# A graph layer on one core: packed adjacency masks turned by VectorE in 32x32 blocks, with row groups in the quadrants

## The chip, the cores and the metric

The kernel runs on one core of one Trainium2 chip. The metric is device time in microseconds (us), from the first to the last thing the program does; the median of three runs before the change is 190.73 (190.70 to 190.74). A core has five engines that work at the same time, each through its own queue in order: PE (TensorE, matrix multiplication), DVE (VectorE), ACT (ScalarE), POOL (GpSimd) and SP (SyncE, which here only issues DMAs).

## The reference

Inputs are `x` (4096 x 64), an adjacency matrix `adj` (4096 x 4096, float32, zeros and ones), a weight (64 x 64) and a bias (64).

```python
h = jnp.maximum(_layernorm(x, axis=-1), 0.0)
support = h @ weight
mask = (adj != 0).astype(support.dtype)
rank = jnp.cumsum(mask, axis=1)
deg = rank[:, -1:]
k = jnp.minimum(deg, 100.0)
pos = rank - (deg - k)
w = mask * jnp.where(pos > 0, 0.5 ** (k - pos), 0.0)
out = x + (w @ support + bias)
```

Since `k - pos = deg - rank`, the weight of a neighbour is one half to the power of the number of neighbours to its right in the row, and zero from the hundredth on. So for each row the kernel counts ones from the right, makes a weight of each, and multiplies by `support`. `adj` is 67.1 MB and is read once.

## The kernel before

**Units.** The 4096 rows are 32 row tiles of 128 (a tile takes every sixteenth row of one half of the matrix, so that each partition's x rows are contiguous). Four row tiles make a row group `g` of W = 512 rows, and each group is done in two column halves of 2048 columns, the right one first: 16 units, 64 loads of 1 MB (`load`, L115, a ring of NA = 8 buffers of 8 KB a partition).

**From mask to weights.** For each load, `convert` (L330) turns float32 into bytes 64 or 65 and puts four columns into one 32-bit word: DVE does 61 of 64, ACT three. `transpose` (L344) turns the words, 128 x 128 at a time, on PE into PSUM, four per load; `settle` (L354) copies them back to SBUF on DVE. Columns are now on the partitions, rows on the free axis, 512 rows side by side. For each unit, `totals` (L365, eight matmuls into 32-row strips) counts the ones of blocks of columns; the count comes as two bytes, which `split` (ACT, L378) and `divide` (DVE, L381) take out; for a left half, `carry` (POOL, L387) adds what the right half found; `suffix` (L390, two matmuls) sums over the blocks to the right; `clamp` (DVE, L398) limits the sum. `place` (L402) makes, for four PSUM banks at a time, the exponents of all columns: four matmuls of 32 rows with `where`, then sixteen of 32 x 32 with the triangle `tri`. `weigh` (ACT, L415) takes an exponential of two bytes of each word: 128 x 1024 weights from one bank. `aggregate` (L445) multiplies them into a 128 x 512 accumulator, two matmuls of 512 columns per weigh, with `support` split into a high and a low part (`hr`) as the stationary side.

**Ends.** `drain`, `turn_back` and `finish` (L462 to L486) add the bias, turn a row group back, add x in SBUF. In the last unit three weighs are done by DVE instead (`encode`, `take`, with `lower` on POOL and `gather` on PE) and three are cut into halves of 256 rows. Two large stores wait for all loads to be issued; the last two go out from ACT's and SP's queues.

**Set-up.** x is turned (`turn`, `turned`), normalised (`center`, `square`, `relu`, `spread`, `root`, `power` on POOL), multiplied by the weight (`support`), scaled (`scale`), split (`first`, `second`). `warm` gives PE matmuls without use, where a planned gap is long.

**Order.** A planner at the end of the function (L524 to L657) holds for each step its engine, a rank (with hand-set shifts), an assumed hold and lag, what it needs and which pool it takes a buffer from; it places the steps one by one, and each engine's queue is written in that order. The order is fixed when the program is built; at run time each instruction waits for its own semaphores. PSUM has two banks for counts and turns (NB), five for `place` (NV) and one for the accumulator.

Of the kernel before, what the change touches and what calls it, by code (L numbers as in the profile page):

```python
# [29 lines left out]

@with_exitstack
def kernel(
# [14 lines left out]

# [7 lines left out]
    CB = HB // E  # L74
# [4 lines left out]
    G = RT // TG  # L79

    UNITS = [(g, c * P * E, n) for g in range(G) for c, n in ((4, 4), (0, 4))]
    U = len(UNITS)
    UT = [(u, tt) for u in range(U) for tt in range(TG)]
    NT = len(UT)
    POS = [sum(UNITS[v][2] for v, _ in UT[:n]) // 2 for n in range(NT + 1)]
    NP = 2 * CB
    QUICK = (U - 2, 4), (U - 1, 0), (U - 1, 4)
    PARTED = 5, 6, 7
    NA = 8
    NV = 5  # L90
    NB = 2
# [4 lines left out]
    bpool = ctx.enter_context(tc.tile_pool(name="bpool", bufs=6))  # L96
    mpool = ctx.enter_context(tc.tile_pool(name="mpool", bufs=3))
    wpool = ctx.enter_context(tc.tile_pool(name="wpool", bufs=NP + 4))
    dpool = ctx.enter_context(tc.tile_pool(name="dpool", bufs=2))
    bhpool = ctx.enter_context(tc.tile_pool(name="bhpool", bufs=3))  # L100
# [7 lines left out]


    tiles = {}  # L110
    xt = mpool.tile([P, CB, W, 2], F16, name="mt").rearrange("p c i e -> p (c i e)").bitcast(F32)
    xr = const.tile([P, H, HT, D], F32, name="xr")
    xr_v = x.rearrange("(r p t) d -> p r t d", r=H, t=HT)

    def load(n):  # L115
        u, tt = UT[n]
        g, c0, cb = UNITS[u]
        t = g * TG + tt
        tiles[n] = apool.tile([P, N // H], F32, tag="a_sb", name="a_sb")
        nc.sync.dma_start(tiles[n][:, :cb * E * P], adj_v[:, t // HT, t % HT, c0:c0 + cb * E * P])  # L120
# [9 lines left out]

# [13 lines left out]

    thr, later, excess = {}, {}, {}
    for cb in sorted({cb for g, c0, cb in UNITS}):
        thr[cb] = setup.tile([P, 4, SUB], F32, name=f"thr{cb}")
        later[cb] = const.tile([P, 2, P], F16, name=f"later{cb}")
        excess[cb] = const.tile([P, 1], F32, name=f"excess{cb}")
        nc.gpsimd.memset(thr[cb], 4096.0)  # L150
        nc.gpsimd.iota(thr[cb][:, :, 4:4 + 4 * cb].rearrange("p j (a f c) -> p j a f c", f=2, c=4),
                       pattern=[[1, 4]] + [[32, 2]] * (cb == CB) + [[16, 2], [4, 4]], base=0, channel_multiplier=0,
                       allow_small_or_imprecise_dtypes=True)
        nc.gpsimd.memset(thr[cb][:, :, 0:1], -1.0)
# [21 lines left out]

# [11 lines left out]
    for q in range(4):  # L188
        nc.gpsimd.memset(band[q * SUB:(q + 1) * SUB, SUB - 4 + q:SUB - 3 + q], 1.0)
    over = setup.tile([P, 1], F16, name="over")  # L190
    nc.gpsimd.memset(over, 136.0)
    floor = const.tile([P, 1], F32, name="floor")
    nc.gpsimd.memset(floor, -38.0 * LN2)
# [4 lines left out]
    used = setup.tile([P, 2], F32, name="used")  # L198

    def order_of(cb):  # L200


        sub = setup.tile([P, 2], F32, name=f"sub{cb}")
        nc.vector.scalar_tensor_tensor(sub[:, 0:1], pf[:, 1:2], 8.0 if cb == CB else 2.0, pf[:, 3:4], op0=ALU.mult, op1=ALU.add)
        nc.vector.scalar_tensor_tensor(sub[:, 0:1], pf[:, 2:3], 0.125, sub[:, 0:1], op0=ALU.mult, op1=ALU.add)
        nc.vector.tensor_scalar(sub[:, 1:2], sub[:, 0:1], 16.0, None, op0=ALU.add)
        nc.vector.memset(sub[:1, 0:1], 4000.0)
        for f in range(2):
            nc.vector.tensor_scalar(later[cb][:, f, :], thr[cb].rearrange("p j r -> p (j r)"), sub[:, f:f + 1], used[:, f:f + 1],
                                    op0=ALU.is_lt, op1=ALU.mult)  # L210

    def constants(n):
        if n == 0:
            nc.vector.tensor_tensor(pi[:, 1:], pi[:, 0:1].to_broadcast([P, 5]), bits, op=ALU.bitwise_and)
            nc.vector.tensor_copy(pf, pi)
            nc.vector.tensor_scalar(used, pf[:, 5:6].to_broadcast([P, 2]), 8.0, None, op0=ALU.is_equal)
            nc.vector.memset(used[:1, 0:1], 1.0)

            nc.vector.tensor_scalar(one, row, 20.0, -1.0, op0=ALU.is_ge, op1=ALU.mult)
        elif n == 1:  # L220

# [15 lines left out]

    hr = const.tile([P, B, 2, D], F32R, name="hr")
    xs = setup.tile([P, B, D], F32, name="xs")
    sq = xs.rearrange("p (b s) d -> p b (s d)", s=2)  # L240
    rx = setup.tile([P, HB, P], F32, name="rx")
# [3 lines left out]
    def warm(n):  # L245

        for i in range(n):
            nc.tensor.matmul(none[:, :2 * P], junk[:, :P], junk, start=True, stop=True)  # L248

    pxs, sqs, ns = {}, {}, {}  # L250

    def turn(h, t0):

        pv = pxs[h, t0] = ps_v.tile([P, P, 4], F32, tag="v", name="px")
        for t in range(4):
            nc.tensor.transpose(pv[:D, :, t], xr[:, h, t0 + t, :], ident)  # L256
# [5 lines left out]
    def center(n):  # L262

        pxs[n] = ps_v.tile([P, W], F32, tag="v", name="pc")
        nc.tensor.matmul(pxs[n], less.rearrange("p h d -> p (h d)"), xt[:, n * W:(n + 1) * W], start=True, stop=True)  # L265


    def groups(of, n):
        return of[:, 4 * n:4 * n + 4, :].rearrange("p j (c l) -> p c j l", l=SUB)

    def square(n):
        nc.scalar.activation(groups(sq, n), pxs[n].rearrange("p (c j l) -> p c j l", c=4, j=4), AF.Square, scale=D ** -0.5)  # L272

    def relu(n):
        nc.scalar.activation(groups(rx, n), pxs.pop(n).rearrange("p (c j l) -> p c j l", c=4, j=4), AF.Relu)
# [8 lines left out]

# [7 lines left out]

# [17 lines left out]
    def piece(h, i):  # L310
        return slice(h * HB + i * HB // 2, h * HB + (i + 1) * HB // 2)

    def first(h, i):
        nc.scalar.activation(hr[:, piece(h, i), 0, :], xs[:, piece(h, i), :], AF.Copy)

    def second(h, i):
        nc.vector.tensor_sub(hr[:, piece(h, i), 1, :], xs[:, piece(h, i), :], hr[:, piece(h, i), 0, :].bitcast(F32))

    def count(cb):
        r = SUB * cb  # L320
        px = pxs["count", cb] = ps_v.tile([P, W], F32, tag="v", name="pn")
        nc.tensor.matmul(px[:, :1], later[cb][:r, 1, :], over[:r], start=True, stop=True)

    def counted(cb):
        nc.vector.tensor_scalar(excess[cb], pxs.pop(("count", cb))[:, :1], one, None, op0=ALU.add)


    low, codes, masks, words, wts, accs, tots, pts, sums8, behind, vs, signed = {}, {}, {}, {}, {}, {}, {}, {}, {}, {}, {}, (1, 7, 15)

    def convert(n):  # L330
        cb = UNITS[UT[n][0]][2]
        m8 = bpool.tile([P, CB * P, E], U8, name="m8")
        m_v, a_v = m8[:, :cb * P, :], tiles.pop(n)[:, :cb * P * E]
        if cb == CB:
            m_v, a_v = m_v.rearrange("p q e -> p e q"), a_v.rearrange("p (e q) -> p e q", e=E)
        else:
            m_v, a_v = m_v.rearrange("p q (a f) -> p a f q", f=2), a_v.rearrange("p (f a q) -> p a f q", f=2, a=2)
        if n in signed:
            nc.scalar.activation(m_v.bitcast(I8), a_v, AF.Sign)  # L339
        else:  # L340
            nc.vector.tensor_scalar(m_v, a_v, 0.0, 64.0, op0=ALU.not_equal, op1=ALU.add)  # L341
        words[n] = m8

    def transpose(n, c0, c1):  # L344
        u, tt = UT[n]
        if tt == 0 and c0 == 0:
            masks[u] = mpool.tile([P, CB, W, 2], F16, name="mt")
        if c0 == 0:
            pts[n] = ps_t.tile([P, CB, P], F32, tag="t", name="pt")
        m32 = words[n].rearrange("p q e -> p (q e)").bitcast(F32)  # L350
        for c in range(c0, c1):
            nc.tensor.transpose(pts[n][:, c, :], m32[:, c * P:(c + 1) * P], ident)  # L352

    def settle(n):  # L354
        u, tt = UT[n]
        cb = UNITS[u][2]
        mw = masks[u].rearrange("p c i e -> p c (i e)").bitcast(U32)[:, :cb, tt * P:(tt + 1) * P]
        pt = pts.pop(n).bitcast(U32)[:, :cb, :]
        words.pop(n)
        if n in signed:  # L360
            nc.vector.tensor_scalar(mw, pt, 0x01010101, 0x40404040, op0=ALU.bitwise_and, op1=ALU.bitwise_or)
        else:
            nc.vector.tensor_copy(mw, pt)  # L363

    def totals(u):  # L365
        tot = pts[u, "n"] = ps_t.tile([P, W], F32, tag="t", name="tot")
        for a in range(2):
            for c in range(UNITS[u][2]):
                nc.tensor.matmul(tot[SUB * c:SUB * (c + 1), :], band[:, SUB - 12 - 4 * a:2 * SUB - 12 - 4 * a],  # L369
                                 masks[u][:, c, :, a], start=(a == 0), stop=(a == 1), skip_group_check=True)  # L370

    def bytes_of(u, f):
        r = SUB * UNITS[u][2]
        if u not in sums8:
            sums8[u] = dpool.tile([P, 2, W], F16, name="sums8")
        return sums8[u][:r, f, :], pts[u, "n"][:r].bitcast(U8).rearrange("p (i f) -> p f i", f=4)[:, 1 + f, :]

    def split(u):  # L378
        nc.scalar.activation(*bytes_of(u, 0), AF.Copy)  # L379

    def divide(u):  # L381
# [313 lines left out]
```

## Time and profile before

| | |
|---|---|
| median of three runs | 190.73 us (190.70 to 190.74) |
| the profiled execution's own time | 190.5 us |
| its span, first to last instruction | 188.8 us |
| mean granted PE clock | 0.979 |
| busy PE / DVE / ACT / POOL | 171.8 / 161.7 / 149.5 / 20.4 us |
| read from memory / written | 68.19 MB / 1.05 MB |
| loads of adj | 64 of 1 MB, median 16.5 us from issue to landing |

Busy times are unions of instruction records; records of one engine overlap, since an instruction may begin before its predecessor has ended. The price of an instruction in a queue is therefore read from start to start of neighbours that waited for nothing. The 40 slices are 4.72 us each.

### The profile page before, as it was taken

How to read it: one execution, taken by the hardware profiler on the slowest of the kernel's cores; microseconds unless marked ns; L12 is line 12 of the kernel's file. 1: busy time of each engine (PE TensorE's matmuls, PEld its weight loads, DVE VectorE, ACT ScalarE, POOL GpSimd, SP SyncE). 2: the span in 40 equal slices, each digit the busy share in tenths (PEclk: the TensorE clock that was granted, in tenths of full speed). 3: DMA queues.
4: the chain of work that ended last, by engine and by line, in shares of the span. 5: the costliest groups of instructions: out<-in, count | busy, mean ns of one | idle time of the engine just before them, and what ended most of it. 6: DMA issues, size and time to landing. Idle time of an engine off the chain costs nothing.

```text
span 188.8 us, 3797 instructions
## 1 busy us (share of the span) xinstructions
PE 171.8 (91%) x1499; PEld 107.7 (57%) x1499; DVE 161.7 (86%) x221; ACT 149.5 (79%) x176; POOL 20.4 (11%) x60
## 2 busy tenths in 40 slices
PE   7879979898989999999979997999799999999980
PEld 5657746655555565466546554655366545554560
DVE  4834758899999999999999989998999899996743
ACT  2298055789899896999897889787978997899970
POOL 7000035020001000100020002000100029001000
PEclk9999687999999999999999999999999999999998
DMA  6999999999999999999999999999999999931000
GB/s 212 417 422 422 415 427 420 417 415 420 420 422 420 420 417 418 429 422 413 422 420 420 422 417 418 420 425 418 420 422 410 424 420 418 418 128 62 21 3 28
DMA packets 10338, 69.49 MB, mean 368 GB/s; under 512 B 1360, under 2 KB 1616, under 8 KB 2128
## 3 DMA queue, kind: packets, MB, share of 16 engines
q1 hardware_dynamic: 10016, 69.15, 88.6%
q8 instruction: 12, 0.20, 0.4%
q10 hardware_dynamic: 304, 0.10, 0.2%
q14 instruction: 6, 0.05, 0.1%
HBM read 68.19 MB, written 1.05 MB: 367 GB/s over the span
## 4 chain that ended last, share of the span: by engine, by line
PE 49%; DVE 29%; DMA 10%; ACT 5%; POOL 3%; issue 2%; POOLq 0%; ACTq 0%; DVEq 0%
PE acc L453 18%; DVE m L341 13%; DMA a_sb<-in_adj_dram 10%; PE pt L352 10%; DVE mt L363 6%; PE v L412 4%; PE v L407 4%; ACT wk L420 3%; PE pc L265 2%; PE tot L369 2%; PE pd L281 2%; PE ps L396 2%; DVE behind L400 2%; PE po L476 2%; ACT mt L260 1%
## 5 line engine op out<-in xcount | busy, mean ns | idle before, releaser
L420 ACT ACTIVATE wk<-v 128x1024 fp32r<-128x1024 uint8 (+1 forms) x128 | 120.0, 1015 | 15.3 <-PE v L412 14.9
L341 DVE TENSOR_SCALAR m<-a_sb 128x2048 uint8<-128x2048 f32 x61 | 84.9, 1394 | 4.2 <-DMA a_sb<-in_adj_dram 4.1
L453 PE MATMUL acc<-wk,hr 128*128 128x512 f32 (+1 forms) x256 | 77.7, 421 | 1.1 <-ACT acc_sb L469 0.6
L453 PEld LDWEIGHTS acc<-wk,hr 128*128 128x128 f32 x256 | 43.4, 189 | 18.6 <-issue 6.3
L352 PE MATMUL pt<-ident,m 128*128 128x128 f32 x256 | 41.2, 286 | 6.0 <-DVE m L341 5.4
L363 DVE COPY mt<-pt 128x512 uint32<-128x512 uint32 x61 | 41.7, 685 | 4.3 <-PE pt L352 4.3
L352 PEld LDWEIGHTS pt<-ident,m 128*128 128x128 f32 x256 | 29.7, 145 | 20.6 <-PE acc L453 4.8
L388 POOL COPY sums<-behind 1x512 f16<-1x512 f16 x8 | 6.8, 852 | 129.6 <-ACT sums L379 109.5
L407 PE MATMUL v<-behind,where 32*128 32x512 f16 x128 | 13.7, 383 | 1.5 <-DVE behind L400 1.1
L412 PE MATMUL v<-mt,tri 32*32 32x512 f16 x512 | 14.2, 394 | 0.0
L379 ACT ACTIVATE sums<-tot 128x512 f16<-128x512 uint8 x16 | 9.7, 608 | 3.5 <-PE tot L369 3.5
L400 DVE TENSOR_SCALAR behind<-ps,excess 128x512 f16<-128x512 f32 x16 | 11.9, 745 | 0.1
L382 DVE CAST sums<-tot 128x512 f16<-128x512 uint8 x16 | 10.9, 683 | 1.1 <-ACT sums L379 1.1
L369 PE MATMUL tot<-mt,band 128*32 128x512 f16 x128 | 10.2, 393 | 0.3 <-DVE mt L363 0.3
L396 PE MATMUL ps<-sums,later 128*128 128x512 f16 x32 | 10.0, 396 | 0.2 <-DVE sums L382 0.2
L407 PEld LDWEIGHTS <-where 32*128 32x128 f16 x128 | 3.7, 90 | 10.3 <-issue 9.8
L412 PEld LDWEIGHTS <-tri 32*32 32x32 f16 x512 | 4.4, 88 | 8.7 <-issue 8.7
L248 PE MATMUL none<-junk 128*128 128x256 bf16 x44 | 7.9, 362 | 1.1 <-DVE junk L133 1.1
L260 ACT ACTIVATE mt<-px 64x512 f32<-64x512 f32 x8 | 4.2, 585 | 4.9 <-PE px L256 4.8
L339 ACT ACTIVATE m<-a_sb 128x2048 int8<-128x2048 f32 x3 | 7.6, 2547 | 0.0
L248 PEld LDWEIGHTS <-junk 128*128 128x128 bf16 x44 | 5.6, 129 | 3.4 <-DVE junk L133 1.1
L272 ACT ACTIVATE xs<-pc 128x512 f32<-128x512 f32 x4 | 2.3, 610 | 6.0 <-PE pc L265 6.0
(87 smaller groups left out, 100.6 us busy)
## 6 DMA issues: line engine op xcount, KB each, us to landing
a_sb<-in_adj_dram SPq DMA_DIRECT2D x64, 1024.0 KB, 16.5
xr<-in_x_dram SPq DMA_DIRECT2D x2, 512.0 KB, 6.3
out_dram<-xr SPq DMA_DIRECT2D x1, 512.0 KB, 18.4
out_dram<-xr SPq DMA_DIRECT2D x1, 384.0 KB, 2.3
out_dram<-xr ACTq DMA_DIRECT2D x1, 64.0 KB, 1.6
out_dram<-xr SPq DMA_DIRECT2D x1, 64.0 KB, 1.7
w<-in_L_gnn_weight_dram ACTq DMA_DIRECT2D x2, 16.0 KB, 6.0
bias_sb<-in_L_gnn_bias_dram SPq DMA_DIRECT2D x1, 0.2 KB, 14.1
```

The lines of the kernel that those rows point to most:

```text
L248: nc.tensor.matmul(none[:, :2 * P], junk[:, :P], junk, start=True, stop=True)
L341: nc.vector.tensor_scalar(m_v, a_v, 0.0, 64.0, op0=ALU.not_equal, op1=ALU.add)
L352: nc.tensor.transpose(pts[n][:, c, :], m32[:, c * P:(c + 1) * P], ident)
L363: nc.vector.tensor_copy(mw, pt)
L369: nc.tensor.matmul(tot[SUB * c:SUB * (c + 1), :], band[:, SUB - 12 - 4 * a:2 * SUB - 12 - 4 * a], masks[u][:, c, :, a], start=(a == 0), st ...
L382: nc.vector.tensor_copy(*bytes_of(u, 1))
L396: nc.tensor.matmul(px, later[cb][:r, f, :], sums[:r, f, :], start=(f == 0), stop=(f == 1))
L400: nc.vector.tensor_scalar(behind[u], pts.pop((u, "s")), excess[UNITS[u][2]], float(MAX_NEIGH), op0=ALU.subtract, op1=ALU.min)
L407: nc.tensor.matmul(v, where[q, a, :], behind[u][q, :], start=True, stop=False, skip_group_check=True)
L412: nc.tensor.matmul(vs[u, 4 * a + j][SUB * c:SUB * (c + 1), :], tri[q, q], m, start=False, stop=True, skip_group_check=True)
L420: nc.scalar.activation(wts[u, k][:, :, r], v.bitcast(U8).rearrange("p (i f) -> p f i", f=4)[:, :2, r], AF.Exp, scale=-LN2, bias=-38.0 * LN2)
L453: nc.tensor.matmul(accs[g][:, r], parts.rearrange("p s d -> p (s d)"), wk[:, s, r], start=(k == s == 0 and c0 + cb * E * P == N), stop=(c0 ...
```

## The change

- Masks are turned by DVE: `flip` transposes 32 x 32 blocks of words from SBUF to SBUF, in place of `transpose` on PE and `settle` on DVE. A block stays in its quadrant (32 partitions), so after it a quadrant holds one group of 32 rows, its partitions are word columns, and the 32 column blocks lie on the free axis with the 32 rows of the group.
- Work goes by whole rows: a load is a row tile of 128 x 4096 (2 MB, four buffers of 16 KB a partition; tile 0 in two loads), a piece is a row tile, and counts are made per piece. There are no column halves and no `carry`.
- `totals` has 256 columns a piece in place of 512; `split` takes both count bytes in one ACT instruction, and `divide` goes. `suffix` is one matmul with `near`, one with `rest`, and seven with `far` on a right part of the columns that gets 32 shorter each time.
- `place` fills four banks per piece with both halves of each word (2 x 256 columns); a piece has four `weigh`s of 128 x 1024. A unit is two row tiles; its weights lie in one 32 KB buffer of two, of which the set-up uses one first. `aggregate` has 32 matmuls of 256 columns for each unit.
- Tiles 30 and 31 are one unit of another kind, "columns": quadrants hold quarters of the columns, each load is four DMAs of 32 partitions, tile 31 is cut into two pieces of 64 rows, and all aggregates of the unit wait for the last piece.
- The three conversions on ACT, the three weighs on DVE and the cut weighs go. The last row group is drained in three parts; all stores go out from SP.
- The planner is written anew, with due times set by a table for each step. In the order it builds, there are 20 warm-up matmuls where there were 44; the last DVE steps are: convert tile 30, a clamp, flip, convert both halves of tile 31, clamp of tile 30, flips of both halves, two clamps.

```diff
+UNITS = [("rows", ((t, 0, 4), (t + 1, 0, 4))) for t in range(0, 30, 2)] + [("columns", ((30, 0, 4), (31, 0, 2), (31, 2, 4)))]
+SPANS = {"rows": 8, "columns": 2}
+STEP = {0: 2}
+DRAINS = [(g, 0, 4, True) for g in range(7)] + [(7, 0, 2, True), (7, 2, 3, True), (7, 3, 4, False)]
+STORES = [(0, 0, 16), (1, 0, 12), (1, 12, 14), (1, 14, 15), (1, 15, 16)]
+NA, NM, NT, NW, NV, NB = 4, 4, 4, 2, 5, 2
...
+    quarters = adj.rearrange("(r g p t) (q n) -> r t q p g n", r=H, g=E, t=HT, q=E)
...
+        if kind == "rows":
+            nc.sync.dma_start(tiles[t][:, k0 * N // 4:k1 * N // 4], adj_v[:, t // HT, t % HT, k0 * N // 4:k1 * N // 4])
+        else:
+            to = tiles[t].rearrange("(q p) (g n) -> q p g n", q=E, g=E)
+            for q in range(E):
+                nc.sync.dma_start(to[q, :, k0:k1, :], quarters[t // HT, t % HT, q, :, k0:k1, :])
...
-            nc.tensor.transpose(pts[n][:, c, :], m32[:, c * P:(c + 1) * P], ident)
...
-            nc.vector.tensor_copy(mw, pt)
...
+    def flip(n):
+        u, i, k0, k1 = LOADS[n]
+        kind, pieces = UNITS[u]
+        k = 2 * (k1 - k0)
+        if (u, i) not in masks:
+            masks[u, i] = mpool.tile([P, 4, W // 2, 2], F16, name="mt")
+        to = masks[u, i].rearrange("p c i e -> p c (i e)").bitcast(F32)[:, :, :width(u, i)]
+        m_v = words.pop(n).rearrange("p q e -> p (q e)").bitcast(F32)[:, :k * P].rearrange("p (k c l) -> p k c l", c=4, l=SUB)
+        if kind == "rows":
+            nc.vector.transpose(to.rearrange("p c (h r) -> p h c r", r=SUB)[:, 2 * k0:2 * k1], m_v)
+        else:
+            to = to.rearrange("p c (h g r) -> p h g c r", h=2, r=SUB)
+            g0 = pieces[i][1]
+            for h in range(2):
+                nc.vector.transpose(to[:, h, k0 - g0:k1 - g0], m_v[:, h::2])
...
+        nc.scalar.activation(sums8[u, i][:, :, :w], pts.pop((u, i, "n"))[:, :w].bitcast(U8).rearrange("p (i f) -> p f i", f=4)[:, :2, :],
+                             AF.Copy, bias=-136.0)
...
+        todo = [(px[:, :w], near, one8), (px[:, :w], rest[kind], all8)]
+        n = w // SPANS[kind]
+        todo += [(px[:, :w - d * n], far[kind], all8[:, d * n:]) for d in range(1, SPANS[kind])]
+        if kind == "columns":
+            todo += [(px[:, n:w], past, all8[:, :n])]
...
+                nc.tensor.matmul(vs[u, i, j][:, a * w:(a + 1) * w], where[q, a, :], behind[u, i][q, :w],
+                                 start=(a == 0), stop=False, skip_group_check=True)
...
+                nc.tensor.matmul(vs[u, i, j][SUB * c:SUB * (c + 1), :2 * w], tri[q, q],
+                                 masks[u, i][q, c, :w, :].rearrange("p i a -> p a i"), start=False, stop=True, skip_group_check=True)
...
+            nc.tensor.matmul(accs[g][:, at:at + 2 * P], hr[:, b, :, :].rearrange("p s d -> p (s d)"), w, start=(k == m == 0),
+                             stop=(k == 7 and m == 3), skip_group_check=True)
```

In the planner, a unit of the kind "rows" lets its aggregates wait for the last weigh of its second piece; the weighs of unit 1 wait for all four steps of `second`, since their buffer held the set-up's data.

## The prediction

> **What bounds the kernel now.** I read the page first (engines and the 40 slices), then busy time by stage, then the timelines of ScalarE, VectorE and of the end.
>
> ```profile
> span 188.8 us, 3797 instructions
> ...
> PE 171.8 (91%) x1499; PEld 107.7 (57%) x1499; DVE 161.7 (86%) x221; ACT 149.5 (79%) x176; POOL 20.4 (11%) x60
> ...
> DMA  6999999999999999999999999999999999931000
> GB/s 212 417 422 422 415 427 420 417 415 420 420 422 420 420 417 418 429 422 413 422 420 420 422 417 418 420 425 418 420 422 410 424 420 418 418 128 62 21 3 28
> ```
>
> See two stretches. From slice 2 to slice 35 the DMA moves 420 GB/s without a dip, while no engine stops: a stream. Then the stream ends and some 22 us follow in which almost nothing is moved. PE's 91% is not the bound of the first stretch (overlapping records fill it); a change of PE work counts only through what is still undone when the stream ends.
>
> ```profile
> 140.00:160.00 20.00, 19.59 (x192) 11.65 (x190) 18.64 (x22) 17.35 (x21) 5.21 (x7) 1.00 1.01 418
> 160.00:170.00 10.00, 9.54 (x89) 5.65 (x88) 9.77 (x12) 9.10 (x11) 0.70 (x1) 1.00 0.68 279
> 170.00:180.00 10.00, 9.68 (x98) 5.27 (x98) 7.05 (x10) 9.35 (x12) 0.60 (x1) 1.00 0.10 39
> 180.00:189.00 9.00, 3.93 (x23) 2.93 (x21) 2.97 (x7) 3.11 (x7) 0.00 (x0) 0.93 0.06 16
> ```
>
> Columns: stage, length, busy PE, PEld, DVE, ACT, POOL, clock, DMA share, GB/s. From 170 to 180 PE and ACT are still full: the last unit is 512 rows by 2048 columns (4 MB), so eight weighs and sixteen matmuls of 512 columns come after the last conversion. The time is (end of the stream, 165) + (tail, 23.8).
>
> The prices, from back-to-back rows (start to start):
>
> ```profile
> 94.24 0.60 ACT L379 ACTIVATE sums<-tot 128x512 f16<-128x512 uint8 x1
> 94.72 0.70 ACT L469 ACTIVATE acc_sb<-acc,bias_sb 128x512 f32<-128x512 f32 x1
> 95.29 1.96 ACT L420 ACTIVATE wk<-v 128x1024 fp32r<-128x1024 uint8 x2
> 97.48 3.77 ACT L420 ACTIVATE wk<-v 128x1024 fp32r<-128x1024 uint8 x4 [0.23 <-PE v L412]
> ```
> ```profile
> 95.89 1.38 DVE L341 TENSOR_SCALAR m<-a_sb 128x2048 uint8<-128x2048 f32 x1
> 97.16 0.67 DVE L363 COPY mt<-pt 128x512 uint32<-128x512 uint32 x1
> ...
> 98.68 0.74 DVE L400 TENSOR_SCALAR behind<-ps,excess 128x512 f16<-128x512 f32 x1
> 99.34 1.40 DVE L341 TENSOR_SCALAR m<-a_sb 128x2048 uint8<-128x2048 f32 x1
> ```
> ```profile
> 182.14 0.63 PE L453 MATMUL acc<-wk,hr 128*128 128x256 f32 x4
> ...
> 186.13 0.33 SPq L486 DMA_DIRECT2D out_dram<-xr  x1
> ```
>
> A split costs ACT 0.48, a drain 0.57, a weigh 0.92 (four in 3.77, one of 1.02). A conversion costs DVE 1.27, a clamp of 512 columns 0.66, a settle 0.6. An aggregate matmul of 256 columns costs 0.12 (four in 0.63, one alone lasts 0.28); the chain of waits gives two of 512 columns 0.47, four mask transposes 0.44, eight totals 0.56, two suffixes 0.44; a place starts 0.70 before what follows it (172.50 to 173.20). The last store is issued at 186.13 and the span ends 2.67 later.
>
> [...] VectorE's rows of 4-byte words from PSUM show 1.09 ns an element (0.56 for 512). [...] every load before covers 128 partitions and moved 420 GB/s[...].
>
> **The change, part by part**, in engine time over the run:
> - PE loses 256 mask transposes: 64 x 0.44 = -28. The suffix is no longer 2 matmuls of 512 but 9 of 256 down to 32 columns (1408 in all): 0.59 by columns, 0.65 with seven more weight loads; 31 x 0.65 + 2 x 0.2 against 16 x 0.44: +13.5. Totals 33 x 0.33 against 16 x 0.56: +2. Place 31 x 0.75 + 2 x 0.55 against 32 x 0.7: +2. Aggregate 512 x 0.12 against 256 x 0.235: +1. Together -10. Warm-up matmuls fall from 44 to 20 in the built order; PE's clock averaged 0.69 from 20 to 30 us before, and setting up has slack then, so I give this nothing (bounds 0 and 1 us, in the early wait below).
> - DVE loses 64 settles (-37) and 16 casts of the second count byte (-9.6). The flip of a tile is 1024 words: [...] as the settle's 1.09 ns an element with its fixed part, 1.12, [...] 1.13; 32 x 1.13 = +36. [...] Clamp 31 x 0.39 + 2 x 0.26 against 16 x 0.66: +2. Three conversions come from ACT (3 x 1.27 = +4), three encodes and takes go (-5). Together about -10. A conversion is now one instruction of 2.5, and a clamp or flip can queue behind it that long; before, 1.27.
> - ACT: splits 31 x 0.48 + 2 x 0.27 against 16 x 0.48: +8; three weighs +3; three conversions -8. Together +3.
> - POOL loses carry and lower: off the path before and after.
> - SP: the same bytes. Rows of 16 KB in place of 8 KB; tiles 30 and 31 in 12 DMAs of 32 partitions. The issues (0.33 each) lie in a queue that mostly waits. The ring is 64 KB a partition in both, four tiles now[...].
>
> **Is the stream still the bound?** A tile of 2.1 MB takes 4.9 to 5.0. Per tile DVE needs 2.5 + 1.13 + 0.39 + 0.22 (finish) = 4.24; ACT 4 x 0.92 + 0.48 + 0.14 = 4.29; PE 16 x 0.12 + 0.75 + 0.65 + 0.33 + 0.13 = 3.8. All below. So the cover of every edit above is the stream, and its price is nothing until an engine passes 4.9.
>
> One new wait is early: unit 1's weights reuse the buffer of the set-up, so its weighs wait for the last two "second" subtractions. In DVE's new order these stand behind the conversion of tile 4 (lands about 30) and two flips: 30 + 2.6 + 0.4 + 2.3 + 1.2 = 36.5. Every later weigh is queued behind. From there ACT has 29 x (3.67 + 0.48) + 7 x 0.57 = 124 to the end of tile 30, that is 161 without a wait, against 170 as the loads allow. It may lose 0.32 us a tile.
>
> **The end of the stream.** 68.19 MB are read, 3.22 by 10 us (322 GB/s), the rest at 420: 164.7. [...] I take 427: 162.2. Column loads: from nothing to twice their 9.8 us; I take 0.5, since several MB are in flight at once (16.5 us from issue to landing) and four such DMAs cover all partitions. T = 162.7.
>
> **The tail after T**, in the new order: DVE converts the last half tile (0.2 to 1.5); only behind it stand the clamp of tile 30 (1.9) and both half flips (3.2). Place of tile 30 follows (3.0); ACT, still draining, starts its weighs at 3.5; with two small splits they end at 7.7. Half tile 31a: four weighs of 0.48, to 9.7, a drain, 10. Five PSUM banks let the last place start only after the third of these (9.3), to 10.3. First weigh of 31b at 10.9; now PE is late: the unit's 32 matmuls all wait for its last piece, 32 x 0.12 = 3.9, to 14.8. Then drains on ACT and, behind it, DVE (0.38 each, one PSUM bank), transpose 0.34, finish 0.45, store 2.67: 19. Overlaps I can't place, about -0.7; ACT behind the loads, 0 to 6, I take 1.5. Tail 19.8; span 182.5. The profiled execution took 190.5 for its span of 188.8, so 1.7 more, and the median is 0.2 above: **184.3**.
>
> **Rivals.**
> 1. ACT becomes the bound. Before, it waited 14.9 us for places in 21 waits, one of 2.0; now there are 33 places with the same five banks. At 0.45 a tile: 29 x 0.13 = 3.8 later, about **188**. Against: a split between two sets of weighs covers 0.48 of a place. Range 186.5 to 190.3.
> 2. [...] Then tiles 30 and 31 run at half of 420: +9.8 us, less the 1.5 of lateness that this hides: **192.5**, slower. It decides when the 4.2 MB fall below some 257 GB/s (9.8 + 6.5 us). For: every DMA lies in one quarter of the partitions. Against: what was said above.
> 3. [...] DVE 5.3 a tile, 0.4 over the stream, 30 x 0.4 = 12: **196**.
> 4. [...]
>
> **Chances.** Forecast (181.5 to 186.5) 0.50; [...] ACT bound 0.23, of which 0.03 within 0.2% of before (what a measurement can tell from no change); ports 0.12; flip at half rate 0.05. The range leaves out the last two and a little below: 180.3 to 190.3. Faster 0.80, same 0.03, slower 0.17.
>
> **What would show it.** GB/s of 427 or so to about 163; a flip of 1.1 to 1.2; ACT's waits for place under 0.3 a tile; DVE idle before conversions on the DMA, which is rare now (4.1 us); the rate in the last 10 us of the stream. I am wrong if conversions late in the run no longer wait for a load, or if the last slices of the stream fall to half.

## The result, and the profile after

The changed kernel takes 199.82 us (median of four runs, 198.68 to 200.43) against 190.72 (190.70 to 190.74): ratio 1.047, 95% interval 1.0418 to 1.0522. The forecast was 184.3 and faster; it is 9.1 us slower. The profiled execution took 200.25, its span is 198.0, its mean PE clock 0.914 (0.979 before). Ratios and medians leave out executions over 1.5% above the fastest of the same kernel, and where too few are left only the times are given.

From the page after, the lines that stood first for the kernel before:

```profile
span 198.0 us, 4612 instructions
...
PE 164.3 (83%) x2007; PEld 124.3 (63%) x2007; DVE 152.1 (77%) x169; ACT 153.3 (77%) x195; POOL 9.9 (5%) x46
...
PEclk9995599559999999999999999999999996965899
DMA  6999999999999999999999999999999999830020
GB/s 221 405 434 424 440 424 406 437 427 427 427 420 424 422 430 420 427 424 434 424 424 417 430 417 427 427 430 424 430 417 391 199 223 223 243 118 3 0 93 13
```

PE and DVE lost the work that they were to lose (7.5 and 9.6 us of busy time), and ACT gained 3.8. Read the last two rows together: in slices 32 to 35 the DMA row stays at 9, 9, 9 and 8, but what is moved falls from about 425 to between 199 and 243 GB/s. The engines of the DMA are busy all the time and carry half. Slices are 4.95 us, so the fall begins at about 153 us, where the loads of tiles 30 and 31 begin.

Busy time by stage, columns as in the prediction (stage, length, PE, PEld, DVE, ACT, POOL, clock, DMA share, GB/s):

```profile
140.00:160.00 20.00, 18.00 (x270) 13.58 (x269) 16.89 (x13) 19.86 (x25) 0.00 (x0) 1.00 1.01 344
160.00:170.00 10.00, 7.61 (x82) 6.20 (x81) 4.98 (x6) 7.41 (x9) 0.00 (x0) 0.83 1.01 222
170.00:180.00 10.00, 5.04 (x73) 3.11 (x71) 8.09 (x11) 4.94 (x6) 0.00 (x0) 0.74 0.44 138
180.00:189.00 9.00, 8.73 (x124) 7.38 (x108) 1.91 (x6) 6.86 (x12) 0.00 (x0) 0.72 0.01 2
```

Before, 160 to 170 moved 279 GB/s at a share of 0.68, because the stream ended inside it; now the share is 1.01 at 222, and DVE and ACT stand idle for half and a quarter of the time. DVE's timeline says for what:

```profile
161.03 2.63 DVE L509 TENSOR_SCALAR m<-a_sb 128x4096 uint8<-128x4096 f32 x1 [3.24 <-DMA a_sb<-in_adj_dram]
...
169.90 2.63 DVE L509 TENSOR_SCALAR m<-a_sb 128x4096 uint8<-128x4096 f32 x1 [3.95 <-DMA a_sb<-in_adj_dram]
...
177.30 1.37 DVE L509 TENSOR_SCALAR m<-a_sb 128x2048 uint8<-128x2048 f32 x1 [1.91 <-DMA a_sb<-in_adj_dram]
```

The three are tiles 29 and 30 and the second half of tile 31. The last load lands at 177.2 (issued at 169.8, 7.4 from issue to landing); before, it landed at 167.9 (issued at 150.4, 17.5 to landing): +9.3. What follows takes 20.8, against 20.9. So the difference of the spans, 9.2, lies ahead of the last landing. (The 165 and 23.8 of the prediction count from where the stream would have ended at its full rate, some 3 us ahead of the landing.)

### The profile page after: what moved, and what is told of

Its sections match the earlier page's. It is cut to its first block, busy times and chain, and to the rows that moved or that the text cites. A ratio compares the mean times of both kernels' runs of the same rounds, so it can differ in the third digit from the quotient of the medians.

```text
span 198.0 us, 4612 instructions
## 1 busy us (share of the span) xinstructions
PE 164.3 (83%) x2007; PEld 124.3 (63%) x2007; DVE 152.1 (77%) x169; ACT 153.3 (77%) x195; POOL 9.9 (5%) x46
## 4 chain that ended last, share of the span: by engine, by line
PE 37%; DMA 22%; DVE 17%; ACT 15%; POOL 3%; issue 3%; SPq 1%; POOLq 0%; ACTq 0%; DVEq 0%
PE acc L601 22%; DMA a_sb<-in_adj_dram 22%; ACT wk L584 12%; DVE m L509 8%; PE ps L551 5%; DVE mt L520 4%; PE v L570 3%; PE v L565 3%; PE tot L532 3%; DVE behind L556 2%; POOL t L473 2%; ACT sums L538 1%; PE po L619 1%; ACT acc_sb L611 1%; DVE wk L482 1%
## 5 line engine op out<-in xcount | busy, mean ns | idle before, releaser
L509 DVE TENSOR_SCALAR m<-a_sb 128x4096 uint8<-128x4096 f32 (+1 forms) x34 | 84.0, 2479 | 13.4 <-DMA a_sb<-in_adj_dram 13.4
L601 PE MATMUL acc<-wk,hr 128*128 128x256 f32 x512 | 78.1, 304 | 6.2 <-ACT wk L584 5.4
L601 PEld LDWEIGHTS acc<-wk,hr 128*128 128x128 f32 x512 | 68.6, 203 | 14.6 <-ACT wk L584 7.6
L520 DVE STREAM_TRANSPOSE mt<-m 128x1024 f32<-128x1024 f32 (+1 forms) x31 | 37.1, 1203 | 0.3
L538 ACT ACTIVATE sums<-tot 128x512 f16<-128x512 uint8 (+1 forms) x33 | 20.0, 607 | 14.2 <-PE tot L532 7.8
L556 DVE TENSOR_SCALAR behind<-ps,excess 128x256 f16<-128x256 f32 (+1 forms) x33 | 15.5, 470 | 19.0 <-PE ps L551 17.1
L565 PE MATMUL v<-behind,where 32*128 32x256 f16 (+1 forms) x264 | 16.8, 281 | 12.1 <-DVE behind L556 8.7
L551 PEld LDWEIGHTS <-far_rows 128*128 128x128 f16 x210 | 17.3, 103 | 1.2
L551 PE MATMUL ps<-sums,far_rows 128*128 128x224 f16 (+6 forms) x210 | 17.8, 228 | 0.0
L570 PE MATMUL v<-mt,tri 32*32 32x512 f16 (+1 forms) x528 | 15.3, 413 | 0.0
```

The lines of the kernel that those rows point to most:

```text
L520: nc.vector.transpose(to.rearrange("p c (h r) -> p h c r", r=SUB)[:, 2 * k0:2 * k1], m_v)
L538: nc.scalar.activation(sums8[u, i][:, :, :w], pts.pop((u, i, "n"))[:, :w].bitcast(U8).rearrange("p (i f) -> p f i", f=4)[:, :2, :], AF.Cop ...
L551: nc.tensor.matmul(o, l, m, start=(k == 0), stop=(k == len(todo) - 1), skip_group_check=True)
L556: nc.vector.tensor_scalar(behind[u, i][:, :w], pts.pop((u, i, "s"))[:, :w], excess, float(MAX_NEIGH), op0=ALU.subtract, op1=ALU.min)
L565: nc.tensor.matmul(vs[u, i, j][:, a * w:(a + 1) * w], where[q, a, :], behind[u, i][q, :w], start=(a == 0), stop=False, skip_group_check=True)
L570: nc.tensor.matmul(vs[u, i, j][SUB * c:SUB * (c + 1), :2 * w], tri[q, q], masks[u, i][q, c, :w, :].rearrange("p i a -> p a i"), start=Fals ...
```

## The experiments

There were two theories from the start. *Ports*, a name alone: the loads of 32 partitions run at half rate (rival 2; what in the hardware would do it, no trace of this case shows). *Backlog*: ACT is several tiles behind the stream, so that with the loads repaired the end would still be late (rival 1, by another mechanism than the one I gave it). The trace after speaks for both: ACT is full from 80 to 160, and the last slices are at half rate. In the expectations a kernel named e1, e2 and so on is the run of that number. Where nothing else is said, an edit is made to the changed kernel.

| run | us, median | ratio to before (95%) | profiled span |
|---|---|---|---|
| e1 | 197.5 | 1.0376 (1.0313 to 1.0438) | 195.0 |
| e2 | 206.06, one run | | 204.2 |
| e3 | 197.13, one run | | 195.2 |
| e4 | 205.68 | 1.0792 (1.0737 to 1.0847) | 206.7 |
| e5 | 198.15, one run | | 196.3 |
| e6 | 193.66 | 1.017 (1.0107 to 1.0233) | 189.9 |
| e7 | 198.40 | 1.0398 (1.0304 to 1.0491) | 201.6 |
| e8 | 191.91 | 1.01 (1.006 to 1.0139) | 188.0 |
| e9 | 192.96 | 1.0114 (1.0089 to 1.0139) | 190.4 |
| e10 | 197.06 | 1.0326 (1.0286 to 1.0367) | 195.6 |
| e11 | 188.88 | 0.9896 (0.9877 to 0.9916) | 186.8 |
| e12 | 191.94 to 198.91, four runs | | 193.3 |

### What halves the rate: e1, e2, e3

e1 makes tiles 30 and 31 an ordinary unit of rows:

```diff
-UNITS = [("rows", ((t, 0, 4), (t + 1, 0, 4))) for t in range(0, 30, 2)] + [("columns", ((30, 0, 4), (31, 0, 2), (31, 2, 4)))]
+UNITS = [("rows", ((t, 0, 4), (t + 1, 0, 4))) for t in range(0, 32, 2)]
```

> Tiles 30 and 31 become an ordinary unit of the kind rows, loaded over 128 partitions; the rest of the changed kernel stays. Theory of the ports ([...] that alone put the end of the stream 14.6 us late, with a colder PE behind it): the stream holds 420 to 430 GB/s to its end at about 163, and the time is 183 to 188 us. Theory of short runs (4 KB pieces 8 MiB apart are slow): the same here. Theory of the backlog (ACT and PE, not the stream, set the end): no faster than 195, since the last unit is coarser than before.

e2 and e3 keep e1's computation and cut only the loads of tiles 30 and 31, each into four DMAs: e2 by partitions, e3 by columns.

```diff
+                for q in range(E):       # e2
+                    p = slice(32 * q, 32 * (q + 1))
+                    nc.sync.dma_start(tiles[t][p, :], adj_v[p, t // HT, t % HT, :])
+                for q in range(E):       # e3
+                    c = slice(q * N // 4, (q + 1) * N // 4)
+                    nc.sync.dma_start(tiles[t][:, c], adj_v[:, t // HT, t % HT, c])
```

> As the kernel with rows to the end, but tiles 30 and 31 come in four DMAs of 32 partitions each, with the same runs of 16 KB. Ports: the last 4.2 MB move at 210 to 220 GB/s, the stream ends 9 to 14 us later than with rows over 128 partitions, and the time is 9 to 15 us above it. Short runs: the runs are as long as in the other tiles, so no loss, within 1 us of it.

> As the kernel with rows to the end, but tiles 30 and 31 come in four DMAs of 128 partitions with runs of 4 KB. Ports: 128 partitions again, so the rate stays above 400 GB/s and the time is within 1.5 us of rows to the end. Short runs: 4 KB pieces cost as in the column loads, 5 to 10 us later.

The GB/s rows of e1, e2 and e3, in this order:

```profile
GB/s 230 395 437 427 430 427 412 430 423 430 427 427 430 418 430 420 427 420 423 417 430 427 430 427 423 430 417 430 423 427 417 430 422 297 35 3 80 1 13 15
```
```profile
GB/s 221 373 446 427 430 424 422 427 427 427 420 433 419 424 433 414 430 430 417 430 430 411 440 417 408 424 427 414 446 411 247 220 231 205 107 3 0 77 14 13
```
```profile
GB/s 226 410 438 426 426 430 421 423 426 430 426 426 430 418 430 423 430 423 420 426 423 426 426 430 423 426 423 430 426 423 416 404 403 315 29 3 22 59 15 13
```

e1's stream holds 417 to 430 and ends at about 164, as forecast. The same bytes in runs of 16 KB, but 32 partitions a DMA, fall to 205 to 247 (e2, +9.2 us of span over e1). In runs of 4 KB over all 128 partitions they stay at 403 to 416 (e3, 197.13 in one run, no loss). So it is the 32 partitions of a DMA that halve the rate, not the short runs and not the number of DMAs: what *Ports* says of the rate is shown. But e1 itself comes at 197.5 and not at 183 to 188: with the stream mended, its tail is 31 us long. The time did not follow the stream. e1's end, on ACT and then on PE:

```profile
175.84 1.12 ACT L584 ACTIVATE wk<-v 128x1024 fp32r<-128x1024 uint8 x1
178.87 3.77 ACT L584 ACTIVATE wk<-v 128x1024 fp32r<-128x1024 uint8 x4 [1.91 <-PE v L570]
```
```profile
183.06 1.23 PE L601 MATMUL acc<-wk,hr 128*128 128x256 f32 x4 [3.60 <-ACT acc_sb L611]
184.08 0.63 PE L619 MATMUL po<-ident,acc_sb 128*128 128x128 f32 x2
184.36 5.55 PE L601 MATMUL acc<-wk,hr 128*128 128x256 f32 x28
```

Tile 30's last weigh ends at 177, 13 us after that; then tile 31 is counted, placed and weighed one after the other, and the unit's 32 matmuls, which all wait for it, run at 0.20 each where I had 0.12.

### Can the quarters be mixed: e4, e5

If two half-rate DMAs side by side each kept their rate, the stream would be whole again. e4 issues quarters 2 and 3 on ACT's queue; e5 cuts every quarter into 128 KB and alternates lower and upper quarters on SP's queue.

```diff
-            for q in range(E):
-                nc.sync.dma_start(to[q, :, k0:k1, :], ...)
+            for q in (0, 2, 1, 3):   # e4
+                (nc.sync if q < 2 else nc.scalar).dma_start(to[q, :, k0:k1, :], ...)
+            for g in range(k0, k1):  # e5
+                for q in (0, 2, 1, 3):
+                    nc.sync.dma_start(to[q, :, g:g + 1, :], ...)
```

> The changed kernel with the column loads of the two upper quarters of the partitions issued from the queue of ACT and those of the lower two from SP[...]; bytes, runs and strides are the same. Ports: the last 4.2 MB move at 350 to 430 GB/s, the stream ends at 163 to 166, time 183 to 188 us. Short runs: still 200 to 240 GB/s, time 198 to 201 us. Six issues of some 0.4 us each are added to ACT's queue, 2 us at most.

> The changed kernel with each column load cut into DMAs of 128 KB, one for a row group and a quarter, issued from SP in the order of quarters 0, 2, 1, 3[...]. Ports: [...] the last 4.2 MB move faster than the 215 GB/s of the changed kernel, 250 to 400; time 189 to 197. If the rate stays at 200 to 240, neighbours in one queue do not mix[...].

The GB/s rows of e4 and e5, and the longest wait of ACT in e4 (what waited, total, times, longest):

```profile
GB/s 231 387 431 428 428 434 407 422 441 418 434 418 433 418 415 441 409 441 415 438 418 418 428 425 425 431 422 434 412 304 233 252 250 197 6 0 3 0 89 14
```
```profile
GB/s 226 389 441 427 431 427 412 427 431 434 424 424 422 424 427 421 427 421 427 424 427 427 424 427 424 427 424 421 431 424 417 234 201 220 253 188 3 3 91 15
```
```profile
ACT wk L584 <- DMA a_sb<-in_adj_dram: 14.1, 1, 14.1
```

Neither reaches the full rate: 233 to 252 with two queues, 188 to 253 alternating. e4 is slower by 5.9 than the kernel that it changes, and its trace (of an execution of 208.72) says why: ACT stood 14.1 us behind the DMA issues put into its queue. e5 came at 198.15 in its one run, outside the 189 to 197 that it was to have. From 160 to 170 the two move 256 (e4) and 235 GB/s (e5), against 222 in the changed kernel: 15 and 6% more. My sentence "four such DMAs cover all partitions" supposed that DMAs in flight make up for each other, an estimate that these rates do not bear out.

But e5 does not close the question. Its stage from 160 to 170, and its issues on SP's queue (duration in ns: least, median, most; then first and last start):

```profile
160.00:170.00 10.00, 7.18 (x90) 5.86 (x92) 6.68 (x8) 7.46 (x10) 0.00 (x0) 1.00 0.79 235
```
```profile
L312 SPq DMA_DIRECT2D a_sb<-in_adj_dram x32: 311/419/1521, 147.0 to 171.1; - x32
```

The share is 0.79, so the DMA was not busy all the time as it was in the changed kernel (1.01 at 222): 235 at 0.79 is some 300 GB/s of busy time. And 128 KB in a median issue of 0.419 us cannot come faster than some 310 GB/s, with 12.3 us of waits on top (8.6 for earlier loads, 3.7 for a conversion). So alternating quarters did let the DMA run faster while it was busy, and SP's issues and waits left it idle in between. How far this would go with fewer or cheaper issues was not tested.

### What is left with the loads repaired: e6

e6 keeps every step of the changed kernel, its order and its small pieces at the end, and loads tiles 30 and 31 over 128 partitions, so that only the content of these buffers differs.

```diff
-        if kind == "rows":
+        if True:
             nc.sync.dma_start(tiles[t][:, k0 * N // 4:k1 * N // 4], ...)
```

> The changed kernel, every step in its order, but tiles 30 and 31 are loaded over 128 partitions as in the other units, with the same bytes in the same pieces. The unit of columns then works on masks in the wrong arrangement, so the last 256 rows are not those of the reference; the work is the same. Theory of the ports alone (only the late loads failed in the prediction): stream ends at 163 to 164, span 182 to 185, time 184 to 187. Theory of the backlog (ACT leaves the set-up some six tiles behind the stream, needs 4.33 us a tile for each, and ends tile 30 near 177 whatever the loads do): time 190 to 193.

The last 256 rows are then worked out from masks in another arrangement. 193.66: the half-rate loads cost 6.2 us of time (199.82 to 193.66), although the last load lands 11 earlier (166.2 for 177.2). The rest is covered by ACT. Stages of e6:

```profile
30.00:40.00 10.00, 4.67 (x53) 2.93 (x53) 9.78 (x9) 5.58 (x8) 0.00 (x0) 0.63 1.01 424
40.00:60.00 20.00, 17.37 (x206) 13.61 (x205) 17.61 (x13) 14.40 (x18) 0.00 (x0) 0.84 1.01 426
60.00:80.00 20.00, 17.36 (x221) 12.94 (x220) 15.62 (x13) 17.05 (x21) 0.00 (x0) 0.91 1.01 426
80.00:100.00 20.00, 17.95 (x240) 13.56 (x239) 18.30 (x15) 19.42 (x24) 0.00 (x0) 1.00 1.00 424
...
170.00:180.00 10.00, 8.45 (x140) 6.59 (x139) 4.63 (x11) 10.00 (x16) 0.00 (x0) 1.00 0.01 2
```

Nothing is moved from 170 on, and ACT is full: it works off old tiles. The time was lost in the first three stages shown, where ACT gets 5.6 of 10, 14.4 of 20 and 17.0 of 20; in the first of them DVE has 9.8 of 10 us of work and PE only 4.7. From 80 on ACT is full, and no conversion waits for a load: the chain is catching up, at 4.43 us a tile (the weighs of tile 15 begin at 106.6, those of tile 27 at 159.7) against 4.92 for the stream, and has not finished when the stream ends. DVE, through which every tile must pass first, is nearly as full (19.3 of 20 us from 120 to 140). ACT's timeline of e6 in the bad stretch (in brackets: idle before, and what ended it):

```profile
38.26 0.60 ACT L538 ACTIVATE sums<-tot 128x512 f16<-128x512 uint8 x1 [3.06 <-PE tot L532]
39.82 3.77 ACT L584 ACTIVATE wk<-v 128x1024 fp32r<-128x1024 uint8 x4 [0.96 <-DVE hr L492]
43.46 0.62 ACT L538 ACTIVATE sums<-tot 128x512 f16<-128x512 uint8 x1
45.65 7.51 ACT L584 ACTIVATE wk<-v 128x1024 fp32r<-128x1024 uint8 x8 [1.56 <-PE v L570]
...
56.29 0.60 ACT L538 ACTIVATE sums<-tot 128x512 f16<-128x512 uint8 x1 [2.64 <-PE ps L551]
```

By 60 us ACT has weighed some five tiles where the stream has brought eleven.

### What makes ACT late: e7, e8, e9

The weighs of unit 1 begin at 39.8 behind a "second" (L492), 3.3 later than I had. e7 gives the last two seconds an earlier rank on e6's base; e8 leaves the order alone and puts 28 zero matmuls into the idle stretch of PE before the first aggregates; e9 is e8 with the two seconds moved by hand to before the conversion of tile 4.

```diff
-    "second": [-417, 143, 783, 704],
+    "second": [-417, 143, -500, -500],      # e7
```
```diff
+        if (u, k) == (0, 0):                # e8, e9: in aggregate
+            for i in range(28):
+                nc.tensor.matmul(accs[g][:, at:at + 2 * P], junk[:, :P], junk, start=True, stop=True, skip_group_check=True)
...
+    late = [s for s in steps if s[3:] in (("second", (1,)), ("second", (3,)))]     # e9: in the planner's list
+    n = next(i for i, s in enumerate(steps) if s[3:] == ("convert", (5,)))
```

> As the kernel with columns fed by rows (the last 256 rows again not the reference's), and the last two second subtractions stand in front of the conversion of tile 4 on DVE instead of behind two conversions and two flips, so that unit 1's weighs can begin at 35 to 36 us instead of 40.2. Backlog: ACT is ahead by what it gained, the end comes 2 to 5 us earlier than without the edit. Ports alone: the stream sets the end, no change within 0.5 us.

> As the kernel with columns fed by rows (the last 256 rows not the reference's), plus 28 matmuls of zeros into the accumulator ahead of the first aggregate, which fill the gap of 4.6 us that PE has there from about 31.3 us. Theory of the cold PE (work was taken from PE, so it stands idle, its granted clock falls to half from 33 to 43 us, and the places that ACT waits for come late): PE's clock from 30 to 40 rises from 0.63 to over 0.9, ACT's first weighs after unit 1 begin 2 to 3 us earlier, the end comes 2 to 4 us earlier, time 190 to 192. Rival (the early wait of unit 1's weighs for the second subtractions alone holds ACT): no change within 0.7 us.

> As the filled kernel, and the last two second subtractions are put by hand in front of the conversion of tile 4 on DVE, with every other step in its place (the planner isn't asked again). If both hold ACT back: weighs of unit 1 begin at 36 to 37.5 instead of 40, another 1.5 to 3 us, time 187 to 190. If the cold PE alone: as the filled kernel. If the second alone: the whole gain of 2 to 4 us comes here.

**e7** missed. One rank is no local edit: the planner set other steps anew. PE in e7 (an execution of 203.5, the slowest of four):

```profile
36.38 4.63 PE L601 MATMUL acc<-wk,hr 128*128 128x256 f32 x20 [4.57 <-ACT wk L584]
40.95 0.53 PE L565 MATMUL v<-behind,where 32*128 32x256 f16 x8
```

Twenty aggregates now stand before the place that ACT waits for, after 4.57 us of idleness, and take 0.23 each in place of 0.12: ACT waits 5.6 us there. e7 says nothing on its question, but it shows PE at nearly half its speed after standing idle ("cold").

**e8** fills this idle stretch. PE's first aggregates in e6 and in e8, and ACT's second set of weighs in e12, which has the same filler:

```profile
35.25 1.22 PE L601 MATMUL acc<-wk,hr 128*128 128x256 f32 x4 [4.57 <-ACT wk L584]
```
```profile
34.80 0.74 PE L604 MATMUL acc<-wk,hr 128*128 128x256 f32 x4 [1.51 <-ACT wk L584]
```
```profile
45.53 7.51 ACT L584 ACTIVATE wk<-v 128x1024 fp32r<-128x1024 uint8 x8 [1.13 <-PE v L570]
```

The clock from 30 to 40 rises from 0.63 to 0.88, ACT's second set of weighs starts at 44.58 for 45.65, and the weighs at 64.60 start at 62.63. The median falls by 1.8 (1.6 with all seven executions of e8), a little less than was expected, and the runs overlap (190.37 to 193.01 against 192.16 to 194.86). That the filler made ACT earlier is not shown: in e12 the clock from 30 to 40 is 0.97, and the second set starts at 45.53, as in e6 and in e1 (45.48), which have no filler. What the two timelines show of PE is that the four matmuls took 1.22 after 4.57 us of idleness and 0.74 after 1.51.

**e9** brought nothing over e8: 192.96. The seconds are no longer what the weighs wait for, and unit 1 still starts at 40.17:

```profile
39.68 0.60 ACT L538 ACTIVATE sums<-tot 128x512 f16<-128x512 uint8 x1 [4.29 <-PE tot L532]
40.17 3.77 ACT L584 ACTIVATE wk<-v 128x1024 fp32r<-128x1024 uint8 x4
```

Now the split waits 4.29 for totals, because the flip of that tile slid behind the two seconds: DVE has 10.00 of 10 us of work from 30 to 40. Inside a full engine the order seems only to choose which wait is seen. My step "the second at 36.5" named the right place, but not its cause.

### Is it really ACT: e11

e11 is e8 with ACT relieved by half of every split (the second count byte is left out of the sums) and nothing else made shorter:

```diff
-        nc.scalar.activation(sums8[u, i][:, :, :w], ....rearrange("p (i f) -> p f i", f=4)[:, :2, :],
+        nc.scalar.activation(sums8[u, i][:, 0, :w], ....rearrange("p (i f) -> p f i", f=4)[:, 0, :],
```

> The kernel of e8 (all tiles loaded over 128 partitions, 28 filler matmuls) with the split taking only the first of its two count bytes; the suffix's matmuls read a constant zero block in place of the second, so this leaves the second count byte out of the sums (and the last 256 rows are not the reference's, as in e8). ACT loses 256 of the split's 512 elements, about 0.21 us a tile, some 6.5 us over 31 tiles; nothing else gets shorter. Backlog theory (ACT runs at 4.33 us a tile behind a stream of 4.92, and the tail starts when ACT has caught up): the end comes 3 to 6.5 us earlier than e8's 192.0, 186 to 189. If the stream's end or PE's tail sets the end, the time stays at 191 to 193.

A split takes ACT 0.27 in e11 (157.88 to 158.15) and 0.48 in e8 (158.76 to 159.24), so that the 0.21 a tile was right. 188.88 (188.27 to 189.02): 3.0 below e8, and the two ratio intervals lie apart. The expected gain was 3 to 6.5; it lies at the lower end. Stages of e11, and one conversion:

```profile
80.00:100.00 20.00, 18.41 (x254) 13.73 (x245) 18.38 (x14) 19.48 (x25) 0.00 (x0) 0.97 1.01 427
100.00:120.00 20.00, 18.44 (x245) 14.56 (x242) 15.82 (x15) 16.93 (x22) 0.00 (x0) 0.95 1.01 425
120.00:140.00 20.00, 18.99 (x276) 14.52 (x272) 19.28 (x17) 18.40 (x24) 0.00 (x0) 1.00 1.01 425
```
```profile
156.39 2.67 DVE L512 TENSOR_SCALAR m<-a_sb 128x4096 uint8<-128x4096 f32 x1 [0.52 <-DMA a_sb<-in_adj_dram]
```

ACT idles 3.1 of the 20 us after 100, where e6 idled 0.9; its longest wait is 2.41 us, for a place, before 104.35. It has not caught up with the stream there, since tiles still come 4.4 apart (104.3 to 157.0 for tiles 15 to 27): from 100 on it is no longer ACT's own work that holds the chain, and DVE or PE, with 19.3 and 19.0 of 20 us of work from 120 to 140, may be what does. At 156.39 a conversion waits for its load, which none does in e6 after 25 us: only there is the lateness used up, and beyond it less ACT work can gain nothing. So ACT's lateness is shown as a cost of some 3 us in e8; the parts of DVE and PE in it were not separated.

### The whole computation: e10, e12

e10 and e12 are e1 with fillers: 28 zero matmuls before the first aggregates and 28 after those of unit 14, which puts them before the last 32; e10 also has e9's move, e12 keeps e1's order.

```diff
+        if (u, k) == (U - 2, 7):            # in aggregate
+            for i in range(28):
+                nc.tensor.matmul(accs[g][:, at:at + 2 * P], junk[:, :P], junk, start=False, stop=True, skip_group_check=True)
```

> Rows to the end (right output), with the filled gap, the early second, and 28 matmuls of zeros behind unit 14's aggregates, so that PE isn't cold when the last 32 aggregates start. Against rows to the end (197.5): backlog 4 to 6 us smaller, last 32 aggregates 4 us instead of 6.9; span 185 to 188, time 187 to 190, which would beat the kernel before. If only the tail's fill works: 194 to 195. If none: 197.

> The kernel of e1 (tiles 30 and 31 as rows) with the 28 filler matmuls before the first aggregates and 28 before the last 32 (zero products, nothing left out), and the order of e1 kept, without the move of the two second subtractions that e10 had. If cold TensorE stretches at both ends are worth what the traces suggest, 1.6 at the start (e6 to e8) and 2.5 in the last 32 aggregates (6.9 to 4.3 in e10): 197.5 - 4.1 = 193 to 195. If PE's clock is covered by ACT's and DVE's work, 196 to 198, as e10.

The end of e10, ACT and PE, to be held against the same lines of e1:

```profile
181.97 3.77 ACT L584 ACTIVATE wk<-v 128x1024 fp32r<-128x1024 uint8 x4 [1.91 <-PE v L570]
```
```profile
186.25 0.74 PE L604 MATMUL acc<-wk,hr 128*128 128x256 f32 x4 [0.62 <-ACT acc_sb L617]
186.84 0.38 PE L625 MATMUL po<-ident,acc_sb 128*128 128x128 f32 x2
186.97 3.56 PE L604 MATMUL acc<-wk,hr 128*128 128x256 f32 x28
```

The filler at the end works: the last 32 aggregates take 4.3 us in place of 6.9, and from the start of the last weighs to the end of the span it is 13.6 (e10, and 13.6 in e12) in place of e1's 16.1. In e10 ACT's last weighs start 3.1 later than in e1, so that the time is the same, 197.06. e12's four runs lie between 191.94 and 198.91 and allow no verdict. No version that leaves nothing out came below the kernel before.

## Why the prediction was wrong

**Stream end, T = 162.7: the step that failed.** Two terms made it. The rate of 427 on long rows, my estimate, was nearly right: e1 shows 417 to 430 and a full-rate end at about 164. The term for the column loads, +0.5 of a range 0 to 9.8, was wrong: 4.19 MB at 222 GB/s take 18.9 us, 9 more than at 427. The last bytes were there at 177.2, 14.5 later than T. Of these, 9 are the column loads and 1.3 the rest of the stream. Some 3 more are a smaller slip of the working: it took the full-rate end for the landing of the last load, which in e1 came at 167.4. About one stays open: a store of 512 KB, issued at 170.90, shares the last slices, and SP's queue waited 15.4 us in five waits for earlier loads at the column issues. I had the bound and the rival with its price, and put it at 0.12 for a reason that no number stood behind.

**ACT behind the loads, "0 to 6, I take 1.5": mis-sized too.** With the loads repaired (e6) tile 30's last weigh ends at 177.9; the prediction's own working has it at T + 7.7 = 170.4. Of these 7.5, 3.5 are the last load, which lands at 166.2; the other 4.0 are lateness, inside the bound but far above what I took. The step "36.5, then 124 us without a wait" failed twice: the start is 39.8 (+3.3), and ACT then idles 8.6 us between 40 and 80 and 3 from 80 to 170, which makes 176 of the 161. The working checked each engine per tile in the steady state, where ACT's 4.29 was nearly right (4.43 from tile to tile), and never summed DVE's work around 30 to 40, where conversions, flips, seconds and set-up fill it. At 0.5 us of slack a tile a loss of 10 us takes 20 tiles to make up.

**Warm-ups at nothing: open.** e8's filler, which is not the one removed, came with 1.8 us in runs that overlap, against a bound of 1, and e12 shows no earlier weighs from it. What the runs do show is that I asked what the removed filler did before and not what the emptied PE would do after: it stands 4.57 us ahead of the first aggregates.

**Tail 19.8: 20.8**, near, but for partly other reasons. The last 32 aggregates take 4.05 (3.9 forecast). A block of 16 ahead of them, from 180.76, however, took 3.8, where 0.12 each gives 1.9: the PEclk row is down to 6 and 5 about there, after waits for loads (the clock from 178 to 184 is 0.50). That other terms were shorter is luck.

**Prices: right.** Start to start, after (a clamp, a flip, and the conversion between neighbours):

```profile
142.68 0.48 DVE L556 TENSOR_SCALAR behind<-ps,excess 128x256 f16<-128x256 f32 x1
143.08 1.23 DVE L520 STREAM_TRANSPOSE mt<-m 128x1024 f32<-128x1024 f32 x1
144.24 2.60 DVE L509 TENSOR_SCALAR m<-a_sb 128x4096 uint8<-128x4096 f32 x1
```

The clamp costs 0.40 (forecast 0.39), the flip 1.16 (1.13): 1.13 ns a word, near the settle's 1.09; rival 3, the flip at half rate, needs twice that and is dead. A weigh is 0.91 to 0.95 (0.92), a warm aggregate 0.12 to 0.13. The cover failed, not the prices under it.

**Rivals.** Rival 2 gave 192.5 because it assumed that little backlog lay beside it. Rival 1 named the right engine with the wrong cause: the waits for place that it priced at 0.45 a tile came to 4.8 us in all in e6 (14.9 before). The last 0.10 of the chances lay on a stream faster than 427 and no lateness, my estimate; e1 shows 417 to 430. Of the 15.5 us between forecast and measurement the repaired loads give back 6.2, less than half. The half-rate loads and lateness together make the result: 6.2 us from these loads, and what is left of e6 over before, 2.9, from ACT's lateness (3.0 of it taken away in e11) less what the change gains.

**Still open:** whether DVE and PE, which work through the same tiles, hold up the catching up as much as ACT; and how the early waits of ACT divide between DVE's load, PE's cold clock and the two PSUM banks for counts (the waits for ps at 56 to 61); no run varied the banks.

## What to carry to other kernels

Here the rate of the stream was a property of each load's shape: when a change alters the partitions of a DMA, price those bytes at the rate of their own shape (205 to 247 GB/s over 32 partitions in e2, 403 to 416 over 128 in e3), and do not assume that DMAs in flight fill each other's gaps (235 and 256 GB/s in e5 and e4, where 222 had been moved). A pipeline that has slack per tile can still be late at its end: add up every engine's work in the first tiles and divide the shortfall by the slack per tile before you call the stream the bound. PE took 1.22 us in e6 for four matmuls after 4.57 us of idleness, and 0.74 in e8, where a filler stood ahead of them: look for such a stretch ahead of work that others wait for, above all at the end, and check that the engines beside it let the gain through.

## What was not expected of the hardware

- Loads of 32 partitions queued one after the other keep the DMA at a share of about 1.0 and move 199 to 247 GB/s, in runs of 4 KB (the changed kernel) or of 16 KB (e2), against 417 to 430 over 128 partitions (e1). The share of busy time alone shows nothing of it; the GB/s row does.
- Issued from two queues, or in pieces of 128 KB from alternate quarters, they move little more (256 and 235 GB/s from 160 to 170, against 222), in the second case at a share of 0.79 (0.95 in the first).
- They hold up their neighbours: tile 29's load over 128 partitions, still under way when they began, landed 18.3 us after its issue; e1's last four loads took 14.5 to 15.7.
- Cutting a 2 MB load into four DMAs of 128 partitions with runs of 4 KB costs little of the rate (403 to 416 for 417 to 430).
- After 4.57 us without work PE took 1.22 us for four matmuls of 256 columns; with 28 small matmuls in the gap, 0.74 (mean clock from 30 to 40: 0.63 in e6, 0.88 in e8). The last 32 took 6.9 us in e1 and, with such a filler ahead, 4.3 in e10.
